# Transpose buffers and queues for the tiles normed as attention ends, the place of q's bias, and the MLP's tile schedule

## The chip, the cores and the metric

The kernel runs on one core of a Trainium2 chip. The metric is the time of one execution on the device, in microseconds (us), as the median of three runs. A core has a matrix engine (TensorE, here PE), three more compute engines (VectorE, DVE; ScalarE, ACT; GpSimd, POOL) and a queue engine (SyncE, SP). Each takes its own instructions in order, and waits for others by semaphores. DMAs are issued by SP, ACT or POOL, and an issue takes time on the queue that issues it. PE's weight loads (PEld) overlap its matmuls.

## The reference

One transformer block with conditioning, in fp32: batch 2, 2048 tokens, 576 channels, 16 heads of 36 channels, an MLP of 2304. Each batch has its own shift, scale and gate rows from a small product with the conditioning vector.

```python
mod = silu(c) @ w_ada + b_ada
sh_msa, sc_msa, g_msa, sh_mlp, sc_mlp, g_mlp = jnp.split(mod, 6, axis=1)
xn = _ln(x, 1e-06) * (1 + sc_msa[:, None, :]) + sh_msa[:, None, :]
qkv = (xn @ w_qkv + b_qkv).reshape(B, N, 3, H, hd)
q, k, v = (qkv[:, :, 0], qkv[:, :, 1], qkv[:, :, 2])
q = _ln(q, 1e-05, qn_g, qn_b)
k = _ln(k, 1e-05, kn_g, kn_b)
attn = softmax(einsum('bqhd,bkhd->bhqk', q, k) * scale)
o = einsum('bhqk,bkhd->bqhd', attn, v).reshape(B, N, C)
x = x + g_msa[:, None, :] * (o @ w_proj + b_proj)
xn2 = _ln(x, 1e-06) * (1 + sc_mlp[:, None, :]) + sh_mlp[:, None, :]
h = gelu(xn2 @ w1 + b1)
return x + g_mlp[:, None, :] * (h @ w2 + b2)
```

## The kernel before

**Stages.** For each of the two batches: `inputs` (norm of x, q, k and v), `attend` (scores, Exp, values) and `outputs` (the projection and the residual). Then the MLP of both batches together: a first product with Gelu in 72 jobs, and a second product. Tokens go in tiles of 128 (16 a batch) and in blocks of 512 (four a batch).

**A normed tile's way to PE.** PE needs the tile with channels on the partitions, so each tile is turned. `tile_turned` (L886) norms the rows (L272 to L279: statistics on DVE, Sqrt on ACT, a reciprocal and a tensor_scalar on DVE). `squares_turned` (L890) transposes 32 x 32 squares on DVE into a tile named `squares` (L893) and writes it with four DMAs (L898) into a DRAM tile `turned`, in which the squares come to stand in their transposed places. `turned_loaded` (L903) reads it back with three DMAs (L906, L908), and `turned_modulated` (L910) applies scale and shift, on ACT (L915, L391, L392) and POOL (L393). There is one `squares` buffer, so a transpose waits until the four DMAs of the tile before have read it.

**inputs** (L941). Tile by tile: the products q and k (L1028 and L1030), then `next_rows(t + 2)` (L1064), which norms and turns the tile two ahead, then the biases of q and k (`biased`, L1065 and L1066), the head norms, and the product v with its bias. DVE's instructions keep the written order here; those of SP, ACT and POOL are ordered by the planner, and DVE's first instructions of batch 1's inputs may come before the last of batch 0's attention.

**attend** (L1104). Scores on PE (L1122), Exp on ACT (L1126, 128x512 a time), values on PE (L1135), which DVE adds into `ot` (L1181 first, L1183 after). In `finish` (L1144) SP writes the row of softmax sums to DRAM (L1149) and reads it back onto 64 partitions (L1150) into `den`; DVE takes the reciprocal (L1154) and multiplies (L1155), and SP copies the result into `qo` (L1160). Hooks run at given steps. Toward the end `rows_opened` loads the rows of the next stage's first tiles, `measure` takes their statistics (L1219), and at the last step `rows_turned` (L1367) calls the `turn` of `rows_begun` (L1206): one Sqrt and one reciprocal for all tiles, then for each tile the tensor_scalar (L1227) and `squares_turned` (L893, L898, on POOL's queue). At the end of batch 0's attention these are two tiles of batch 1, at the end of batch 1's five tiles for the MLP. In attend DVE, POOL and ACT keep the written order, and the hook stands ahead of the last `ot` eviction. The rows lie in `spare` tiles, slices of `kr` (the keys), which is no longer used by then.

**outputs** (L1245). Sixteen tiles in groups of four: the parts of the projection that do not need the last channels come first (`whole`, L409), then those that do (`halved`, L420), then DVE multiplies by the gate (L1259) and adds the residual (L1266), and POOL stores (L1267) and loads (L1254). With batch 1's outputs go the loads of the MLP's first weights: SP issues four `wb` loads (L1443), between them the reads of the five turned tiles (L906, L908), and then `last_rows` (L1451), which DVE casts and splits (L403, L404) between two products of the outputs. Again DVE keeps the written order.

**MLP.** A job is two 128-wide slices of the hidden channels (9 such pairs) for one of eight blocks of 512 tokens: seven products of half blocks (L1537), the last channels (L1551), and on DVE the additions that combine the seven (L1564 to L1571), with a copy (L1563) and Gelu (L1575) on ACT and a store on SP (L1576). Two sets of PSUM banks alternate, so that job j + 2 needs the evictions of job j. `token_sums` (L1504) makes four sums of a block's input, before its first job. `ahead(job)` (L1578) prepares the next block's tiles: tile i of block m + 1 is loaded at job 2i - 4 of block m, normed and turned at 2i - 2, read at 2i and modulated at 2i + 1; block 1's tile 0 is one of the five tiles of attention's end, and its tile 1 is loaded ahead of the first job. Here DVE keeps the written order.

Of the kernel before, what the change touches and what calls it, by code (L numbers as in the profile page):

```python
# [8 lines left out]
F32 = mybir.dt.float32  # L9
# [7 lines left out]
P = 128  # L17
# [14 lines left out]
def dit_block(  # L32
# [25 lines left out]
    nc = tc.nc  # L58
    B, N, C = x.shape
# [7 lines left out]
    NBLK = N // BLK  # L67
    TPB = BLK // P
# [17 lines left out]
    def s_tile():  # L86
        return psum["s"].tile([P, 2, 512], F32, tag="s", name="s")
# [35 lines left out]
    def halves(ap):  # L123
        return ap.rearrange("p (a f) -> p a f", a=2)
# [159 lines left out]
    with psum_pools(), tc.tile_pool(name="ada", bufs=2) as ada:  # L284
# [19 lines left out]
        turned = s_tile()  # L304
# [30 lines left out]
    x1_dram = dram.tile([B, N, C], F32, name="x1_dram")  # L335
# [49 lines left out]
    def affine(which, k, b):  # L385
        return dict(bias=mod[:, which, k, b : b + 1], scale=mod[:, which + 1, k, b : b + 1])
# [368 lines left out]
    def block_of_small():  # L755
# [3 lines left out]
        xs = {}  # L759
# [126 lines left out]
        def tile_turned(xt, queue):  # L886
            rows_normed(xs["pool"], xt, repeated=False)
            return squares_turned(xt, queue)

        def squares_turned(xt, queue):  # L890

            squares = xs["pool"].tile([P, C], F32, name="squares", bufs=1)
            nc.vector.transpose(squares, xt[:, :C])  # L893
            xs["count"] = xs.get("count", 0) + 1
            turned = dram.tile([C, P], F32, name=f"turned{xs['count']}")
            by_square = turned.rearrange("(k d) (g j) -> g d k j", d=SQ, j=SQ)
            for g in range(P // SQ):
                queue.dma_start(  # L898
                    out=by_square[g], in_=squares[g * SQ : (g + 1) * SQ, :].rearrange("p (k j) -> p k j", j=SQ)
                )  # L900
            return turned

        def turned_loaded(dst, cols, turned, queue):  # L903

            full, parts, _ = dst
            queue.dma_start(out=full[:, :, cols], in_=turned[0:512, :].rearrange("(k p) n -> p k n", p=P))  # L906
            for r0 in (0, 64):
                queue.dma_start(out=parts[r0 : r0 + 64, 1, cols].bitcast(F32), in_=turned[512:576, :])  # L908

        def turned_modulated(dst, cols, which, b):  # L910

            full, parts, _ = dst
            for k in range(FULL):
                part = full[:, k, cols]
                nc.scalar.activation(part, part, AF.Identity, **affine(which, k, b))  # L915
            last_modulated(dst, cols, parts[:, 1, cols].bitcast(F32), which, b)

        def input_turned(b, t, queue):
            return tile_turned(tile_loaded(x[b, t * P : (t + 1) * P, :], queue), queue)
# [6 lines left out]
        def input_modulated(b, xnt):  # L926
            turned_modulated(xnt, slice(0, P), 0, b)
            return xnt
# [12 lines left out]
        def inputs(b, weights, work, xnt, rows, loaded):  # L941

            wq, wq4, bq = weights
            normed, squares, taken = {}, {}, []
# [72 lines left out]
            def next_rows(t):  # L1017
                return tile_turned(loaded.pop(0), nc.gpsimd) if loaded else input_turned(b, t, nc.gpsimd)
# [14 lines left out]
            def biased(w, ps, t, both):  # L1033
                bias = halves(bq[:, w * C : (w + 1) * C])
                if w < 2:
                    nc.vector.tensor_tensor(halves(both[:, w * C : (w + 1) * C]), ps[:, :, :HALF], bias, ALU.add)
                else:
                    heads = "p a (h d) -> p a h d"
                    nc.vector.tensor_tensor(
                        vv[:, t, :, 0:HD].rearrange("p (a h) d -> p a h d", a=2),  # L1040
                        ps[:, :, :HALF].rearrange(heads, d=HD),
                        bias.rearrange(heads, d=HD),
                        ALU.add,
                    )
# [4 lines left out]
            for t in range(NT - 2):  # L1049


                both = work.tile([P, 2 * C], F32, name="both", bufs=3)
                turning = b == t == 0
                if turning:
                    q, k = (product(w, xnt, None, (0,)) for w in range(2))
                    for w, ps in enumerate((q, k)):
                        product(w, xnt, ps, (1,))
                    ahead = second_by_feature(rows)
                else:
                    ahead = input_loaded(rows, nc.gpsimd)  # L1060
                    q = product(0, xnt)
                    k = product(1, xnt)
                    input_modulated(b, ahead)
                rows = next_rows(t + 2)  # L1064
                biased(0, q, t, both)  # L1065
                biased(1, k, t, both)  # L1066
                if t > 0:
                    head_scale(t - 1, before)
                v = product(2, xnt)
                biased(2, v, t, both)  # L1070
                if t >= 2:
                    by_feature(t - 2, banks_of_two())
                centred(both)
                before, xnt = both, ahead


            for t in range(NT - 2, NT):
                both = work.tile([P, 2 * C], F32, name="both", bufs=3)
# [125 lines left out]
        spare = [kr[:, c, a * 640 : a * 640 + C] for c in range(4) for a in range(3)]  # L1204

        def rows_begun(tiles):  # L1206

            st = xs["pool"].tile([P, 2, 6], F32, name="st", bufs=2)
            mv = xs["pool"].tile([P, len(tiles), 2], F32, name="mvs", bufs=1)
            rstd = xs["pool"].tile([P, len(tiles)], F32, name="rstds", bufs=1)  # L1210

            def load(i):
                xt, src = tiles[i]
                not_sooner(xt)
                nc.gpsimd.dma_start(out=xt, in_=src)

            def measure(i):
                for a in range(2):
                    nc.vector.bn_stats(st[:, a, :], tiles[i][0][:, a * HALF : (a + 1) * HALF])  # L1219
                nc.vector.bn_aggr(mv[:, i, :], st.rearrange("p a s -> p (a s)"))  # L1220

            def turn():
                nc.scalar.activation(rstd, mv[:, :, 1], AF.Sqrt, bias=eps6)
                nc.vector.reciprocal(rstd, rstd)
                turned = []
                for i, (xt, _) in enumerate(tiles):
                    nc.vector.tensor_scalar(xt, xt, mv[:, i, 0:1], rstd[:, i : i + 1], ALU.subtract, ALU.mult)  # L1227
                    turned.append(squares_turned(xt, nc.gpsimd))
                return turned

            return load, measure, turn
# [79 lines left out]
        for b in range(B):  # L1311
# [43 lines left out]
                (3 + t // NBLK, t % NBLK, 3): lambda t=t: residual_begun(b, t) for t in range(NT + 1)  # L1355
            }
            if b + 1 < B:
                begun = [(spare[9 + t], x[b + 1, t * P : (t + 1) * P, :]) for t in range(2)]
            else:
                begun = [(spare[3 + j], x1_dram[0, j * P : (j + 1) * P, :]) for j in range(TPB + 1)]  # L1360

            def rows_opened():
                opening["begun"] = rows_begun(begun)
# [25 lines left out]
            if b + 1 < B:  # L1389
# [28 lines left out]
        HF = NF // 2  # L1418
        MH = MLP // 2
        PAIR = 2 * P  # L1420
        NB = B * NBLK
# [3 lines left out]
        xnts = [  # L1425
            (
                mx.tile([P, FULL, BLK], F32, name=f"xnt{i}"),
                mx.tile([P, 2, BLK], F32R, name=f"parts{i}"),
                mx.tile([P, P], F32, name=f"tail{i}"),
            )  # L1430
            for i in range(2)
        ]
# [9 lines left out]
        for i, (k, f) in enumerate(((0, 0), (0, 1), (1, 0), (1, 1))):  # L1442
# [4 lines left out]
            for j in (2 * i, 2 * i + 1):  # L1447
                if j <= TPB:
                    n, t = divmod(j, TPB)
# [16 lines left out]
        def mlp_loaded(n, i, queue):  # L1466
            b, blk = divmod(n, NBLK)
            t0 = blk * BLK + i * P
            return tile_loaded(x1_dram[b, t0 : t0 + P, :], queue)

        between = {}
        for j in range(TPB + 1):
            n, i = divmod(j, TPB)
# [104 lines left out]
        def ahead(job):  # L1578


            n, f = divmod(job, HF)

            def at(offset):
                m, g = divmod(job - offset, HF)
                there = m + 1 < NB and g % 2 == 0 and g // 2 < TPB and (m, g) > (0, 0)
                return (m + 1, g // 2) if there else None

            if todo := at(-4):
                rows_ahead[todo] = mlp_loaded(*todo, nc.gpsimd)
            if todo := at(-2):  # L1590
                rows_ahead[todo] = tile_turned(rows_ahead[todo], nc.gpsimd)
            for offset in (0, 1):
                if todo := at(offset):
                    m, i = todo
                    cols = slice(i * P, (i + 1) * P)
                    if offset == 0:
                        turned_loaded(xnts[m % 2], cols, rows_ahead.pop(todo), nc.gpsimd)
                    else:
                        turned_modulated(xnts[m % 2], cols, 2, m // NBLK)

        for m, k, n in ((2, 0, 0), (5, 1, 1), (3, 0, 1), (4, 1, 0)):
            quarter = w2[k * HF * P : (k + 1) * HF * P, n * HALF : (n + 1) * HALF]
# [10 lines left out]
            nc.sync.dma_start(out=hidden[q % len(hidden)], in_=gelus[n][g])  # L1613

        rows_ahead = {}
        rows_ahead[1, 1] = mlp_loaded(1, 1, nc.gpsimd)
        token_sums(0)
        for job in range(0, NB * HF, 2):
            (n0, f0), (n1, f1) = divmod(job, HF), divmod(job + 1, HF)
# [156 lines left out]
```

## Time and profile before

| what | us |
| --- | --- |
| median of three runs | 3218.88 (3217.01 to 3221.77) |
| the profiled execution | 3216.34 |
| its span | 3214.6 |
| PE busy | 3159.8 (98%) |
| DVE busy | 1510.3 (47%) |
| ACT busy | 1515.2 (47%) |
| POOL busy | 673.1 (21%) |
| mean granted TensorE clock | 0.995 of full |

All the views below are of one profiled execution, which took 3216.34; times in them are microseconds from the start of the span. A busy share is an average over all stages. A wait is named after the instruction that waited and the work that released it, with the sum over the places, their number and the longest. The granted clock is a share of TensorE's full speed. The longest parts of PE's time are the values (935.0 for L1135) and the scores (567.9 and 424.0 for L1122); the q, k and v products take 403.8 (L1028). The squares writes are 248 DMAs of 72 KB, 2.3 from issue to landing in the median.

### The profile page before, as it was taken

How to read it: one execution, taken by the hardware profiler on the slowest of the kernel's cores; microseconds unless marked ns; L12 is line 12 of the kernel's file. 1: busy time of each engine (PE TensorE's matmuls, PEld its weight loads, DVE VectorE, ACT ScalarE, POOL GpSimd, SP SyncE). 2: the span in 40 equal slices, each digit the busy share in tenths (PEclk: the TensorE clock that was granted, in tenths of full speed). 3: DMA queues.
4: the chain of work that ended last, by engine and by line, in shares of the span. 5: the costliest groups of instructions: out<-in, count | busy, mean ns of one | idle time of the engine just before them, and what ended most of it. 6: DMA issues, size and time to landing. Idle time of an engine off the chain costs nothing.

```text
span 3214.6 us, 47348 instructions
## 1 busy us (share of the span) xinstructions
PE 3159.8 (98%) x17833; PEld 1895.2 (59%) x17833; DVE 1510.3 (47%) x2213; ACT 1515.2 (47%) x2951; POOL 673.1 (21%) x946
## 2 busy tenths in 40 slices
PE   8999999999999999999999999979999999999999
PEld 6884333333333788633333333347888888777777
DVE  5774333333333477633333333435566554455454
ACT  2436666666666033467666666632555652000000
POOL 4551000121110255300001111032333320111121
PEclk9999999999999999999999999989999999999999
DMA  5222212233221422121222222246544533333331
GB/s 151 73 65 68 77 48 56 62 82 81 70 72 48 156 69 73 39 61 35 48 58 64 62 72 63 66 151 209 159 133 135 145 107 126 138 133 111 118 103 38
DMA packets 150585, 291.51 MB, mean 91 GB/s; under 512 B 29891, under 2 KB 82444, under 8 KB 148236
## 3 DMA queue, kind: packets, MB, share of 16 engines
q1 hardware_dynamic: 105012, 175.48, 17.9%
q0 software_dynamic: 45328, 112.92, 13.4%
q8 instruction: 143, 2.34, 0.3%
q14 instruction: 94, 0.77, 0.1%
q10 hardware_dynamic: 8, 0.00, 0.0%
HBM read 155.42 MB, written 84.63 MB: 75 GB/s over the span
## 4 chain that ended last, share of the span: by engine, by line
PE 95%; DMA 3%; DVE 1%; SPq 0%; ACT 0%; issue 0%; POOL 0%; DVEq 0%; ACTq 0%; POOLq 0%
PE b L1135 28%; PE b L1122 19%; PE s L1688 15%; PE s L1028 11%; PE m L1537 11%; PE s L409 3%; PE m L1551 2%; PE one L1537 2%; PE s L1030 2%; PE s L988 1%; DMA last_rows<-in_w_dram 1%; DMA gelu<-cs 0%; DMA bq<-in_w_qkv_dram 0%; PE s L420 0%; DMA turned<-squares 0%
## 5 line engine op out<-in xcount | busy, mean ns | idle before, releaser
L1126 ACT ACTIVATE pt<-b 128x512 f32<-128x512 f32 x2048 | 1057.7, 608 | 484.9 <-PE b L1135 270.5
L1135 PE MATMUL b<-pt,vt 128*64 128x512 f32 x4096 | 935.0, 598 | 2.4 <-ACT pt L1126 2.4
L1135 PEld LDWEIGHTS b<-pt,vt 128*64 128x64 f32 x4096 | 271.8, 136 | 584.6 <-issue 439.4
L1122 PE MATMUL b<-qm,km 32*128 32x512 f32 x4096 | 567.9, 614 | 0.3 <-DMA km<-qo 0.3
L1183 DVE TENSOR_TENSOR ot<-b,ot 128x512 f32<-128x512 f32 x192 | 132.7, 691 | 643.2 <-PE b L1135 642.8
L1122 PE MATMUL b<-qe,ke 16*128 16x512 f32 x2048 | 424.0, 790 | 0.0
L1028 PE MATMUL s<-wq,xnt 128*128 128x288 f32 x1536 | 403.8, 406 | 4.8 <-ACT xnt L391 2.7
L1688 PE MATMUL s<-ws,as 128*128 128x288 f32 x1440 | 351.8, 406 | 0.0
L1122 PEld LDWEIGHTS b<-qm,km 32*128 32x128 f32 x4096 | 192.0, 184 | 269.9 <-ACT pt L1126 206.3
L1028 PEld LDWEIGHTS s<-wq,xnt 128*128 128x128 f32 x1536 | 280.1, 190 | 66.3 <-ACT xnt L391 2.9
L1688 PEld LDWEIGHTS s<-ws,as 128*128 128x128 f32 x1440 | 273.6, 190 | 75.6
L898 POOL DMA_DIRECT2D turned<-squares x248 | 167.0, 679 | 391.1 <-DVE squares L893 368.4
L1154 DVE RECIPROCAL den<-den 128x512 f32<-128x512 f32 x64 | 213.6, 3337 | 13.8 <-DMA den<-den_dram 13.8
L1537 PE MATMUL m<-xnt,wb 128*128 128x256 f32 x864 | 210.4, 379 | 3.2 <-DVE cs L1571 2.3
L1537 PE MATMUL m<-s,wb 128*128 128x256 f32 x864 | 210.0, 379 | 0.0
L1181 DVE COPY ot<-b 128x512 f32<-128x512 f32 x64 | 44.3, 692 | 332.3 <-PE b L1135 332.3
L1537 PEld LDWEIGHTS m<-s,wb 128*128 128x128 f32 x864 | 164.2, 190 | 22.3
L1122 PEld LDWEIGHTS b<-qe,ke 16*128 16x128 f32 x2048 | 108.4, 184 | 114.5 <-issue 113.2
L1537 PEld LDWEIGHTS m<-xnt,wb 128*128 128x128 f32 x864 | 158.9, 190 | 23.0 <-DVE cs L1571 2.7
L915 ACT ACTIVATE xnt<-xnt,mod 128x128 f32<-128x128 f32 x248 | 102.6, 481 | 138.5 <-DMA xnt<-turned 110.8
L1239 POOL DMA_DIRECT2D kr<-in_x_dram x32 | 17.5, 548 | 715.0 <-DVE met L786 700.2
L1575 ACT ACTIVATE cs<-cs,b_sb 128x512 f32<-128x512 f32 x144 | 98.9, 719 | 115.7 <-DVE cs L1570 94.0
(197 smaller groups left out, 3049.1 us busy)
## 6 DMA issues: line engine op xcount, KB each, us to landing
gelu<-cs SPq DMA_DIRECT2D x144, 256.0 KB
hidden<-gelu SPq DMA_DIRECT2D x16, 2304.0 KB
turned<-squares POOLq DMA_DIRECT2D x248, 72.0 KB, 2.3
den<-den_dram SPq DMA_DIRECT2D x128, 128.0 KB
xnt<-turned POOLq DMA_DIRECT2D x56, 256.0 KB, 3.8
x_dram<-kr POOLq DMA_DIRECT2D x48, 288.0 KB, 2.7
qm<-qo SPq DMA_DIRECT2D x192, 64.0 KB
kr<-in_x_dram POOLq DMA_DIRECT2D x34, 288.0 KB, 3.7
```

The source lines that it names most:

```text
L409: nc.tensor.matmul(outs[a], stationary(k, a), moving(k, a), start=(first and k == 0), stop=(not first and k == FULL - 1),)
L898: queue.dma_start(out=by_square[g], in_=squares[g * SQ : (g + 1) * SQ, :].rearrange("p (k j) -> p k j", j=SQ))
L915: nc.scalar.activation(part, part, AF.Identity, **affine(which, k, b))
L1028: nc.tensor.matmul(out_a, full[:, k, :], wq[:, k, f], start=k == 0, stop=False)
L1122: nc.tensor.matmul(ps, k[r, keys], q[r, :], start=first, stop=not first)
L1126: nc.scalar.activation(pt[:, h, :], banks[2 * c + h], AF.Exp, scale=SCALE)
L1135: nc.tensor.matmul(acc[64 * h : 64 * h + 64, :], vt[:, v0 : v0 + 64], pt[:, h, :], start=pt is pts[0][0], stop=pt is pts[-1][0],)
L1154: nc.vector.reciprocal(den, den)
L1183: nc.vector.tensor_tensor(ot, acc, ot, ALU.add)
L1537: nc.tensor.matmul(out_m[m], wb[:, slot[m], k, f * P : (f + 1) * P], moving[m](k), start=k == 0 and m in (1, 2, 5, 6), stop=k == 1 and m == 1,
L1575: nc.scalar.activation(part, part, AF.Gelu, bias=b1_sb[:, g : g + 1])
L1688: nc.tensor.matmul(ms[m], stationary[m][:, f, :], ws[m][:, f, :], start=(f == 0), stop=(f == HF - 1))
```

## The change

There are three parts.

- `squares_turned` takes a buffer as an argument. The tiles of `rows_begun` are given spare ones: two at the end of batch 0's attention (`spare[7]`, `spare[8]`), five at the end of batch 1's (`spare[8]` to `spare[11]` and `spare[0]`). The four DMAs of tile i are issued by ACT, SP or POOL, as i is 0, 1 or 2 modulo 3. All other tiles use the single buffer and POOL, as before.
- In `inputs` the bias of q comes ahead of `next_rows(t + 2)` on DVE.
- In the MLP tile i is read at job max(0, 2i - 1), so at 0, 1, 3 and 5; it is turned two jobs before that, loaded five before and modulated two after. Ahead of the first job two tiles are loaded and the first of them is normed and turned, before `token_sums(0)`.

```diff
--- before.py
+++ after.py
@@ -887,9 +887,10 @@
             rows_normed(xs["pool"], xt, repeated=False)
             return squares_turned(xt, queue)
 
-        def squares_turned(xt, queue):
-
-            squares = xs["pool"].tile([P, C], F32, name="squares", bufs=1)
+        def squares_turned(xt, queue, squares=None):
+
+            if squares is None:
+                squares = xs["pool"].tile([P, C], F32, name="squares", bufs=1)
             nc.vector.transpose(squares, xt[:, :C])
             xs["count"] = xs.get("count", 0) + 1
             turned = dram.tile([C, P], F32, name=f"turned{xs['count']}")
@@ -1061,8 +1062,8 @@
                     q = product(0, xnt)
                     k = product(1, xnt)
                     input_modulated(b, ahead)
+                biased(0, q, t, both)
                 rows = next_rows(t + 2)
-                biased(0, q, t, both)
                 biased(1, k, t, both)
                 if t > 0:
                     head_scale(t - 1, before)
@@ -1210,7 +1211,7 @@
             rstd = xs["pool"].tile([P, len(tiles)], F32, name="rstds", bufs=1)
 
             def load(i):
-                xt, src = tiles[i]
+                xt, src, _ = tiles[i]
                 not_sooner(xt)
                 nc.gpsimd.dma_start(out=xt, in_=src)
 
@@ -1223,9 +1224,9 @@
                 nc.scalar.activation(rstd, mv[:, :, 1], AF.Sqrt, bias=eps6)
                 nc.vector.reciprocal(rstd, rstd)
                 turned = []
-                for i, (xt, _) in enumerate(tiles):
+                for i, (xt, _, squares) in enumerate(tiles):
                     nc.vector.tensor_scalar(xt, xt, mv[:, i, 0:1], rstd[:, i : i + 1], ALU.subtract, ALU.mult)
-                    turned.append(squares_turned(xt, nc.gpsimd))
+                    turned.append(squares_turned(xt, (nc.scalar, nc.sync, nc.gpsimd)[i % 3], squares))
                 return turned
 
             return load, measure, turn
@@ -1355,9 +1356,12 @@
                 (3 + t // NBLK, t % NBLK, 3): lambda t=t: residual_begun(b, t) for t in range(NT + 1)
             }
             if b + 1 < B:
-                begun = [(spare[9 + t], x[b + 1, t * P : (t + 1) * P, :]) for t in range(2)]
+                begun = [(spare[9 + t], x[b + 1, t * P : (t + 1) * P, :], spare[7 + t]) for t in range(2)]
             else:
-                begun = [(spare[3 + j], x1_dram[0, j * P : (j + 1) * P, :]) for j in range(TPB + 1)]
+                begun = [
+                    (spare[3 + j], x1_dram[0, j * P : (j + 1) * P, :], spare[(8 + j) % len(spare)])
+                    for j in range(TPB + 1)
+                ]
 
             def rows_opened():
                 opening["begun"] = rows_begun(begun)
@@ -1580,23 +1584,25 @@
 
             n, f = divmod(job, HF)
 
-            def at(offset):
-                m, g = divmod(job - offset, HF)
-                there = m + 1 < NB and g % 2 == 0 and g // 2 < TPB and (m, g) > (0, 0)
-                return (m + 1, g // 2) if there else None
-
-            if todo := at(-4):
-                rows_ahead[todo] = mlp_loaded(*todo, nc.gpsimd)
-            if todo := at(-2):
-                rows_ahead[todo] = tile_turned(rows_ahead[todo], nc.gpsimd)
-            for offset in (0, 1):
-                if todo := at(offset):
-                    m, i = todo
-                    cols = slice(i * P, (i + 1) * P)
-                    if offset == 0:
-                        turned_loaded(xnts[m % 2], cols, rows_ahead.pop(todo), nc.gpsimd)
-                    else:
-                        turned_modulated(xnts[m % 2], cols, 2, m // NBLK)
+            def at(**offsets):
+                for i in range(TPB):
+                    read = max(0, 2 * i - 1)
+                    for what, offset in offsets.items():
+                        m, g = divmod(job - read - offset, HF)
+                        if g == 0 and m + 1 < NB and (m, i) > (0, 0):
+                            yield what, (m + 1, i)
+
+            for what, todo in at(turn=-2, read=0, modulate=2, load=-5):
+                m, i = todo
+                block, cols = xnts[m % 2], slice(i * P, (i + 1) * P)
+                if what == "load":
+                    rows_ahead[todo] = mlp_loaded(*todo, nc.gpsimd)
+                elif what == "turn":
+                    rows_ahead[todo] = tile_turned(rows_ahead[todo], nc.gpsimd)
+                elif what == "read":
+                    turned_loaded(block, cols, rows_ahead.pop(todo), nc.gpsimd)
+                else:
+                    turned_modulated(block, cols, 2, m // NBLK)
 
         for m, k, n in ((2, 0, 0), (5, 1, 1), (3, 0, 1), (4, 1, 0)):
             quarter = w2[k * HF * P : (k + 1) * HF * P, n * HALF : (n + 1) * HALF]
@@ -1613,7 +1619,9 @@
             nc.sync.dma_start(out=hidden[q % len(hidden)], in_=gelus[n][g])
 
         rows_ahead = {}
-        rows_ahead[1, 1] = mlp_loaded(1, 1, nc.gpsimd)
+        for i in (1, 2):
+            rows_ahead[1, i] = mlp_loaded(1, i, nc.gpsimd)
+        rows_ahead[1, 1] = tile_turned(rows_ahead[1, 1], nc.gpsimd)
         token_sums(0)
         for job in range(0, NB * HF, 2):
             (n0, f0), (n1, f1) = divmod(job, HF), divmod(job + 1, HF)
```

## The prediction

> **What bounds the kernel now.** First the page: how busy is TensorE?
>
> ```profile
> PE 3159.8 (98%) x17833; PEld 1895.2 (59%) x17833; DVE 1510.3 (47%) x2213; ACT 1515.2 (47%) x2951; POOL 673.1 (21%) x946
> ```
>
> Of a span of 3214.6 us PE idles 54.8, and no other engine is above 47%: the change can win only what PE idles, and what PE's clock loses after idling. So next PE's waits, by the line that waited and what it waited for (sum, times, longest).
>
> ```profile
> PE s L420 <- DVE ot L1183: 14.1, 1, 14.1
> PE s L306 <- DVE x_first L279: 8.4, 1, 8.4
> PE s L420 <- DVE product L1259: 7.6, 2, 4.5
> PE s L409 <- DVE ot L1183: 4.8, 1, 4.8
> PE s L1028 <- ACT xnt L391: 2.7, 1, 2.7
> PE b L1135 <- ACT pt L1126: 2.4, 1, 2.4
> PE m L1537 <- DVE cs L1571: 2.3, 2, 1.5
> ```
>
> L1183 is attention's last eviction, and it keeps PE twice, at the ends of attention: 14.1 in batch 1 (2120.62 to 2134.70), 4.8 in batch 0 (1036.5 to 1041.33). DVE's waits in 2105 to 2185 say why it is late:
>
> ```profile
> DVE squares L893 <- DMA turned<-squares: 17.7, 4, 5.3
> DVE wr L403 <- DMA last_rows<-in_w_dram: 11.3, 1, 11.3
> ```
>
> Four of five transposes wait for the DMAs of the tile before, which must have read the one squares buffer. Then the chain that ended last, over the same stretch (start, duration, what):
>
> ```profile
> 2113.72 2.14 DMA turned<-squares
> 2116.03 0.79 DVE squares L893
> ...
> 2133.29 0.78 DVE squares L893
> 2134.07 0.59 DVE ot L1183
> 2134.99 2.18 DMA den_dram<-ot
> 2137.24 3.57 DMA den<-den_dram
> 2140.83 3.36 DVE den L1154
> ...
> 2153.69 26.24 DMA last_rows<-in_w_dram
> 2179.96 0.76 DVE wr L403
> ...
> 2182.94 1.33 PE s L420 x4
> ```
>
> The eviction stands behind the last transpose, and the chain runs on: last_rows, which SP issues after the softmax's copies and four wb loads, lands at 2179.96 and keeps PE a second time (4.5). Last, stretches just after these stalls (busy time of five engines, then PE's granted clock, DMA share, GB/s):
>
> ```profile
> 2135.00:2139.00 4.00, 4.00 (x11) 2.47 (x10) 0.00 (x0) 1.47 (x4) 2.02 (x4) 0.55 0.70 202
> 2158.00:2162.00 4.00, 4.00 (x13) 2.44 (x14) 3.36 (x5) 0.00 (x0) 1.72 (x4) 0.63 1.02 395
> 2183.00:2187.00 4.00, 4.00 (x11) 2.56 (x12) 3.96 (x3) 0.00 (x0) 0.83 (x2) 0.58 0.47 147
> ```
>
> Four microseconds at 0.55 lose 1.8 more: a stall from 3 us up costs some 2 us beside itself.
>
> **What the skill says.** "TensorE: Matmul & The Clock Gate", HAM oscillation, wants no PE-idle gap above about 3.4 us, or the clock halves. The trace agrees after 14.1, 4.8 and 4.5; it also shows 0.63 after a stall of 3.09, and no dip after 2.7. "DMA: Bandwidth & Descriptors", Issuing engines are not separate DMA queues: more issuing engines save only issue time. Here four issues on POOL take 2.65 and the last lands 2.14 later, so issue is half of such a turn-round. "ScalarE: Activation LUTs", What ACT_TABLE_LOAD costs: 2.66 a switch with its drain; this trace has 1.28 for the load itself.
>
> **The change part by part.**
>
> *A, batch 0's end.* Each tile has a buffer, so the two (L1227, L893) pairs run at 1.32 each from 1031.5 and the eviction ends near 1035, before PE wants it at 1036.5. Tiles 0 and 1 took 15.49 from 1032.38; the same two, undisturbed, took 7.96 in batch 1. Gain 7.5: 4.8 of stall, the rest clock. The four writes that move to ACT and the four to SP find both queues empty there: ACT's next work, the modulates, needs those writes anyway, and SP's next, den's copy, needs the eviction.
>
> *B, q's bias ahead of the next norm.* At 985.25 the scheduler had pulled batch 1's tile-2 norm into batch 0's attention: Sqrt's and then Exp's table load on ACT, and PE waited 2.40 for pt. In the changed program's compiled order this norm stands behind q's bias, which needs PE's product after the outputs, so it cannot be pulled there. Gain 2.4. It then comes two tiles (26.4 us of PE) before its use, and takes about 15: norm with table load 4.07, writes 5.0, read 3.8, modulate. In the other tiles the norm moves behind one DVE instruction, at nothing: PE runs back to back at 13.2 a tile and covers it; without this cover each us late would cost a us in each of 30 tiles. At startup v waited 2.7 for ACT (L391), which stood behind this norm's Sqrt; it then waits for v's weights, still landing near 33. Gain 0.5, between 0 and 2.4.
>
> *C, batch 1's end.* Five pairs back to back from 2110.0: squares ready at 2111.4 to 2116.7, eviction done near 2117.3, before PE's 2120.6. The 14.1 go. What is late next? SP now carries two of the five tiles' writes. The last is issued near 2118.7 (four at 0.5 after 2116.7), lands near 2121, and SP's first read of a turned tile waits for all of them; den's two reloads queue behind it, near 2122.5. Adding 3.57 (den), 3.36 (reciprocal) and 0.76 (multiply): 2130.6, against 2144.98 before, 14 sooner. ACT's eight issues come after its last Exp and Sqrt and before modulates that need these writes: nothing. POOL keeps four issues of twenty and reaches its loads of x sooner: nothing lost. DVE does two products ahead of that reciprocal; both are ready before den lands. SP's following issues (L1160 x5, L908, wb x4) keep their order and lengths, so last_rows is issued near 2140 and lands near 2166.5. PE, from 2110.93 at its undisturbed 18.1 per 4 tiles, arrives near 2157 and waits until 2166.5 + 2.98 (cast, add, product, as from 2179.96 to 2182.94) = 2169.5. From there the end is 28.2 away, as before: 2197.7 against 2211.15. Gain 13.4, not the 14.1 + 7.6 + clock that the waits promise. Bounds: 5 if last_rows' landing is set by traffic rather than by its issue; 27.6 (100.2 less 72.6 undisturbed) if last_rows stops binding.
>
> *D, the MLP's start.* Tile (1,1)'s norm, 2.97 on DVE, now precedes token_sums(0), ending near 2216.2 in the old clock of the trace. PE's m=5 wants the first sum at 2214.71 and gets it near 2216.9: a wait of 2.2. The wait of 1.45 at 2241.72 (a gelu store behind the ws loads) has a fixed end and absorbs as much. Loss 0.8; 3 if the clock dips too.
>
> *E, three places with two norms in a row.* Loading and turning at jobs 0, 1, 3, 5 instead of 0, 2, 4, 6 puts two norms back to back on DVE ahead of the evictions of jobs 16, 34 and 52 (compiled order). The MLP kept its single squares buffer, so the second transpose waits for the first's writes. With T the end of the eviction before: first squares T + 4.07, written 5.0 later (L898 to L906 at 2250.80 and 2280.03), second transpose to T + 9.9, eviction (2.6) to T + 12.4. PE, which ended job 15 some 2.9 before T, has two jobs of 7.0 to do meanwhile and wants this eviction at T + 11.1. Loss 1.3, say 1.5 with the semaphores, three times: 4.5; between 0 and 9.
>
> *Loads one job sooner:* 0. PE's 7.0 a job hides them before and after; no MLP wait names xt.
>
> Sum: -7.5 - 2.4 - 0.5 - 13.4 + 0.8 + 4.5 = -18.5. The profiled execution took 3216.34 (span and 1.7 around it), so 3197.8; the median of the runs lies 2.54 higher: 3200.4.
>
> **The rivals.** *The traffic binds (R1).* last_rows lands 26 after its issue, so bytes, not issue, may set it. For: DMA share 1.02 in 2158 to 2162. Against: until 2135 the share is 0.19, and nothing new is put ahead of it. C gains 5: 3208.8. *No bound left (R2).* The whole 27.6: 3186. For: the DMAs are spread earlier. Against: the 26.24. *The MLP loses it (R3, slower).* E's price is 1.3 + (d - 5.0), d from squares to turned, plus about 2 of clock once the stall passes 3. Slower by over 0.2% needs (23.0 + 6.4)/3 = 9.8 a place, d from 11.5. For: d was 10.75 once, at 2291.85, beside a 2.3 MB hidden load. Against: that load lies near job 11, not at 16, 34 or 52. At d = 13, (1.3 + 8 + 2) x 3 = 33.9 against the 23.0: 3230. *Nothing happens (R4).* The eviction may still end behind something on DVE; against it, no transpose in the changed order waits for a DMA there. 3219.
>
> **How the numbers follow.** Forecast 0.55, R1 0.18, R2 0.12, R3 0.10, R4 0.05. 0.2% is 6.4 us, about what this measurement can tell from no change. Faster: 0.55, 0.12 and 0.15 of R1, so 0.82; R3 is split 0.06 slower, 0.04 within, with R4 and the rest of R1 0.12 within. The forecast's own range is 3192 to 3208 (E 0 to 9, startup, C by 3). With R1 and half of R2 it is 3187 to 3213, which leaves out 0.2.
>
> **What would show it.** A and C: no PE wait on L1184 (the eviction's new line). C: last_rows landing near 2156 on the changed kernel's clock (2166.5 less the 10.4 that A and B win earlier), one PE wait of 10 to 12 on the product at L1260. B: no ACT pt wait. D: PE waits 2 at the first m=5. E: three PE waits of 1 to 2 on cs near jobs 18, 36, 54. Wrong it would be if den's reload on SP is late, if square writes on three queues slow each other, or if a stall above 3 us shows in the MLP.

## The result and the profile after

The changed kernel takes 3206.09 us (median of six, 3201.74 to 3209.03), against 3218.43 (3215.53 to 3221.77) for the kernel before: a ratio of 0.9961, 95% interval 0.9948 to 0.9974. It is 12.3 faster, where 18.5 were forecast; 3206.1 lies inside the stated range of 3187 to 3213, and inside the forecast's own of 3192 to 3208.

In the profiled executions (3209.03, span 3207.2, against 3216.34, span 3214.6) each stage's time can be read from PE's first instruction of the stage to that of the next:

| stage | before | after | difference | forecast |
| --- | --- | --- | --- | --- |
| start, and inputs of batch 0 | 250.5 | 253.2 | +2.7 | -0.5 |
| attention of batch 0 | 781.9 | 780.4 | -1.5 | -2.4 |
| outputs of batch 0 | 79.1 | 71.5 | -7.5 | -7.5 |
| inputs and attention of batch 1 | 999.5 | 999.3 | -0.2 | 0 |
| outputs of batch 1 | 101.1 | 94.5 | -6.6 | -13.4 |
| the MLP's first product | 506.9 | 512.5 | +5.6 | +5.3 |
| its second product | 495.6 | 495.7 | +0.1 | 0 |

These add up to 7.4 and not to 12.3, because the changed kernel's profiled execution is the slowest of its six, 2.9 above their median, and the one of the kernel before lies 2.1 below its median. The first stage differs most from profile to profile: over the nine kernels of this document that have the same code there as the changed one it ended between 249.4 and 253.8. So the medians give the whole, and the profiles say which stage changed.

PE's waits of the changed kernel (sum, times, longest):

```profile
PE s L420 <- DVE product L1260: 17.1, 2, 8.9
PE s L306 <- DVE x_first L279: 8.6, 1, 8.6
PE s L1029 <- DMA wq<-in_w_qkv_dram: 5.5, 2, 3.9
PE m L1541 <- DVE cs L1575: 3.5, 4, 1.5
PE m L1541 <- DVE s L1511: 2.0, 1, 2.0
```

Both waits for attention's last eviction (now L1184) are gone, and so is Exp's. In their place stand two waits at batch 1's outputs, of 8.95 and 8.12, which are not for the eviction but for products that DVE could not reach. DVE's waits over those outputs (2090 to 2185) say why:

```profile
DVE x L1267 <- DMA x<-x_dram: 10.6, 3, 8.9
DVE den L1155 <- DMA den<-den_dram: 10.1, 1, 10.1
DVE wr L403 <- DMA last_rows<-in_w_dram: 9.9, 1, 9.9
```

Nothing waits for squares there any more. The softmax sums `den`, the residual x and last_rows are late instead. The chain that ended last shows where den's lateness begins:

```profile
2109.53 0.79 DVE kr L894
...
2110.68 1.49 SPq L899
...
2113.68 6.00 DMA turned<-kr
...
2120.01 0.39 SPq L907
...
2121.01 0.59 SPq L1152
...
2137.66 27.93 DMA last_rows<-in_w_dram
...
2168.74 1.33 PE s L420 x4
```

SP's square writes take up to 1.9 to issue, and the last lands 6.0 after its issue began. The first read of a turned tile (L907) waits for them, and den's reload (L1152) stands behind that read. The loads of x (L1255) stand on POOL behind the products of the turned tiles (L393), and these wait for the same reads:

```profile
2125.79 0.45 POOL L393 TENSOR_TENSOR parts<-tail,parts 128x128 fp32r<-128x128 f32 x1 [14.21 <-DMA xnt<-turned]
...
2133.76 1.61 POOL L1255 DMA_DIRECT2D x<-x_dram  x3
```

### The profile page after: what moved, and what is told of

Same layout as the page of the kernel before. It is cut to its first block, busy times and chain, and to the rows that moved or that the text cites. A ratio compares the mean times of both kernels' runs of the same rounds, so it can differ in the third digit from the quotient of the medians.

```text
span 3207.2 us, 47334 instructions
## 1 busy us (share of the span) xinstructions
PE 3159.1 (98%) x17833; PEld 1895.6 (59%) x17833; DVE 1510.2 (47%) x2213; ACT 1505.3 (47%) x2941; POOL 657.2 (20%) x922
## 3 DMA queue, kind: packets, MB, share of 16 engines
q0 software_dynamic: 44176, 111.15, 13.4%
## 5 line engine op out<-in xcount | busy, mean ns | idle before, releaser
L1184 DVE TENSOR_TENSOR ot<-b,ot 128x512 f32<-128x512 f32 x192 | 132.7, 691 | 643.3 <-PE b L1136 642.9
L1155 DVE RECIPROCAL den<-den 128x512 f32<-128x512 f32 x64 | 213.5, 3336 | 13.9 <-DMA den<-den_dram 13.9
L899 POOL DMA_DIRECT2D turned<-squares x220 | 147.6, 677 | 222.8 <-DVE squares L894 197.0
L1696 PE MATMUL s<-ws,hidden 128*128 128x288 f32 x576 | 142.3, 406 | 0.0
```

The source lines that it names most:

```text
L899: queue.dma_start(out=by_square[g], in_=squares[g * SQ : (g + 1) * SQ, :].rearrange("p (k j) -> p k j", j=SQ))
L1155: nc.vector.reciprocal(den, den)
L1184: nc.vector.tensor_tensor(ot, acc, ot, ALU.add)
L1696: nc.tensor.matmul(ms[m], stationary[m][:, f, :], ws[m][:, f, :], start=(f == 0), stop=(f == HF - 1))
```

## The experiments

Each has its stages beside it where they matter: "outputs" is batch 1's outputs (101.1 before, 94.5 in the changed kernel), "MLP" its first product (506.9 and 512.5). A stage is read from one profile of each kernel. Kernels with the same code in batch 1's outputs took 93.3 to 95.2 there with the changed kernel's three queues (four kernels), 83.9 to 84.7 with POOL alone (three) and 101.1 to 104.3 with one buffer (three); the MLP's schedule of before took 506.3 to 509.2 (eight). Smaller differences than these say little.

### e1_buffers: own buffers, POOL alone

```diff
- turned.append(squares_turned(xt, (nc.scalar, nc.sync, nc.gpsimd)[i % 3], squares))
+ turned.append(squares_turned(xt, nc.gpsimd, squares))
```

with q's bias and the MLP as before.

> Own transpose buffers at both attention ends, all square writes still on POOL's queue; the rest as before. Theory (the buffer, not the queues, carries the gain): the waits on the last eviction L1184 (14.1 and 4.8) are gone, batch 0's end gains 7.5. In batch 1 twenty issues on POOL take 5 x 2.65 from 1 us after attention's end on PE, the last lands near 16.5 us after it, as late as with three queues (16.5 in the changed kernel), so last_rows lands 61 us after attention's end as there: in all 13 to 15 faster than before, within 2 of the run with three queues. Rival (the queues matter): the reads on SP are later by 4 or more and the gain is 10 or less.

Measured: 3195.82, ratio 0.9936 (0.9922 to 0.9949). That is 21 faster, more than the whole change brings and more than either theory said. Outputs took 84.7, ten less than with three queues; batch 0's outputs took 76.1, 4.6 more. The trace shows something that the expectation had left out: with no square writes on SP, the compiled order of SP is different. SP at batch 1's end (start, duration, what), where PE's attention ended at 2112.11:

```profile
2118.63 0.53 SPq L1151 DMA_DIRECT2D den_dram<-ot  x2
2120.48 1.14 SPq L1152 DMA_DIRECT2D den<-den_dram  x2
...
2132.38 0.53 SPq L1455 DMA_DIRECT2D last_rows<-in_w_dram  x1
2133.29 0.41 SPq L1447 DMA_DIRECT2D wb<-in_w_dram  x1
2133.76 0.45 SPq L907 DMA_DIRECT2D xnt<-turned  x1
```

den goes ahead of all reads of turned tiles, and the planner put last_rows ahead of wb. In the changed kernel, where attention ended at 2104.46, SP has this:

```profile
2106.25 9.34 SPq L899 DMA_DIRECT2D turned<-kr  x8
2115.68 1.81 SPq L1151 DMA_DIRECT2D den_dram<-ot  x2
2120.01 0.39 SPq L907 DMA_DIRECT2D xnt<-turned  x1
2120.45 0.51 SPq L909 DMA_DIRECT2D parts<-turned  x1
2121.01 1.22 SPq L1152 DMA_DIRECT2D den<-den_dram  x2
```

Nor are the writes done much sooner with three queues. Stretches of four microseconds while the writes run, of the changed kernel (the last three columns are PE's clock, DMA share and GB/s):

```profile
2109.00:2113.00 4.00, 4.00 (x19) 2.90 (x19) 1.79 (x3) 0.00 (x0) 2.58 (x5) 1.00 0.97 129
2113.00:2117.00 4.00, 4.00 (x24) 2.94 (x21) 1.42 (x2) 0.00 (x0) 0.00 (x0) 1.00 1.02 223
```

and of e1_buffers:

```profile
2113.00:2117.00 4.00, 4.00 (x18) 3.16 (x17) 3.90 (x7) 0.00 (x0) 4.00 (x7) 1.00 0.55 82
2117.00:2121.00 4.00, 4.00 (x21) 2.89 (x22) 1.51 (x3) 0.00 (x0) 4.00 (x7) 1.00 0.68 106
```

With three queues the sixteen DMA engines are full (share 0.97 to 1.02), and the writes whose landing the profile gives, POOL's four, land 3.6 to 6.1 after the start of their issue, where the twenty of POOL alone take 2.6 in the median. Twenty writes take 14.7 from the first issue to the last landing (2104.97 to 2119.68), against 15.0 for POOL alone (2112.88 to 2127.91).

### e2_ends: part one alone

The buffers and the three queues of the change, all else as before.

> Part one of the change alone: own buffers and three queues. Theory: batch 0's end gains 7.5 and batch 1's end 6.5, as in the changed kernel's trace, 14 in all (3204). SP's eight square writes take 9 us to issue instead of the 4 that were forecast and the last lands 6 us after its issue. Rival (the changed kernel's stages depend on each other): batch 1's end gains the forecast 13.4 here, 21 in all (3197).

Measured: 3201.93, ratio 0.9957 (0.9943 to 0.9971), 15 faster. Batch 0's outputs took 71.5 and batch 1's 94.2: the gain of part one doesn't depend on the other parts, and the rival falls.

### e3_qbias: q's bias alone

```diff
+ biased(0, q, t, both)
  rows = next_rows(t + 2)
- biased(0, q, t, both)
```

> q's bias ahead of the next norm, alone. Theory: no wait of Exp's pt (2.4 gained at batch 0's attention), and at startup v waits for its weights instead of ACT: 3.9 with a clock dip as in the changed kernel's trace, 2.7 lost; no change in all (3218). Rival (that wait for weights differs from run to run and isn't the edit's): startup as before or 0.5 better, 2.4 to 2.9 gained.

Measured: 3215.03, ratio 0.9993 (0.9984 to 1.0001), between the theory and its rival, with an interval that includes no change. Exp's wait of 2.4 is gone and batch 0's attention takes 780.4 instead of 781.9. The startup could not be settled: in the four kernels without this edit the first stage ended at 248.6, 250.1, 250.5 and 254.6 (the last is e1_buffers, which waited 3.5 for the weights too), in the nine with it at 249.4 to 253.8. With the edit, v waited 0.3 to 4.7 for its weights in eight of the nine (in e8_mixed 2.5 for DVE); without it, 2.5 to 2.8 for ACT in three of the four. What the edit costs there is less than the runs differ by.

### e4_mlp: the MLP's schedule alone

The third part of the change's diff and nothing else.

> The MLP's new tile schedule alone, attention ends as before. Theory: 5 slower than before (3223): 2 of wait and 2 of clock at the first job, where the norm is ahead of token_sums, waits of 1.0, 1.0 and 1.5 at the three places with two norms in a row, less the 2.3 of waits that the old schedule had. Rival (these waits come from the changed kernel's other edits): PE's waits in the MLP are those of before, within 1 of it.

Measured: 3224.55, ratio 1.0024 (1.0014 to 1.0035), 7.7 slower. The MLP took 512.1, with the waits of the changed kernel: 1.96 at the first job, then 0.87, 1.01, 0.26 and 0.92 near jobs 18, 36, 38 and 54. So the third part costs by itself what it costs in the whole, some 5. Batch 1's outputs were 3.2 longer too (104.3; e3_qbias had 103.3 with the same code). Batch 0's attention was 1.7 longer as well: after the wait of 2.40 for Exp's pt, which the kernel before has too, the clock dipped here and not there (the last section shows both).

### e5_rows_first: last_rows ahead of wb

From here to e8 the kernels have own buffers and q's bias first, and the MLP's schedule of before.

```diff
+ nc.sync.dma_start(out=last_rows, in_=w1[512:576, :].rearrange("p (a f) -> p a f", a=2))
  for i, (k, f) in enumerate(((0, 0), (0, 1), (1, 0), (1, 1))):
...
- nc.sync.dma_start(out=last_rows, in_=w1[512:576, :].rearrange("p (a f) -> p a f", a=2))
```

> Own buffers, three queues and q's bias as changed, the MLP's schedule as before; on SP last_rows is issued ahead of the four wb loads, all else on SP in the changed kernel's order. Theory (last_rows' place behind 4.6 MB of wb makes the second stall of about 8): that stall and its clock dip are gone, batch 1's outputs take 85 instead of 94.5; the first stall of about 9 stays, since it comes from x's loads and den. Rival (traffic of all kinds sets it): last_rows lands within 3 of before, or the stall only moves to wb, and the outputs take 91 or more.

Measured: 3195.07, ratio 0.9928 (0.9912 to 0.9945). PE's second stall is gone and DVE no longer waits for last_rows. But outputs took 88.3, not 85: the first stall grew from 8.95 to 11.46. DVE's waits there:

```profile
DVE x L1267 <- DMA x<-x_dram: 12.1, 3, 8.5
DVE den L1155 <- DMA den<-den_dram: 10.3, 1, 10.3
DVE wb L1464 <- DMA wb<-in_w_dram: 7.2, 1, 7.2
```

The place of last_rows is worth 6; den and x stay late as they were, and the theory's 85 was missed by 3.

### e6_reads_act: the turned tiles read by ACT's queue

```diff
- turned_loaded(xnts[n], slice(t * P, (t + 1) * P), first[j], nc.sync)
+ turned_loaded(xnts[n], slice(t * P, (t + 1) * P), first[j], nc.scalar)
```

> As the last one, but last_rows behind wb as in the changed kernel, and the turned tiles of batch 1's end read by ACT's queue instead of SP's. Theory (den's reload stands on SP behind the first read, which waits for SP's own slow square writes): den lands about 5 sooner than the 20 us after attention's end of the changed kernel, last_rows is issued 8 or more sooner than its 33 and the outputs take 86 to 90. Rival (SP's eight square writes alone hold den_dram and so den): den within 2 of before and the outputs 92 or more.

Measured: 3197.29, ratio 0.9934 (0.9917 to 0.995); outputs 89.5. The time is the theory's, the mechanism only in part: den was there 17.8 after attention's end, 2.5 sooner and not 5, and last_rows was issued at 31.1, 2 sooner and not 8. Its cast began 21.4 after that issue instead of 27.9; why is not shown. PE had one stall of 14.0 there, while DVE waited 16.0 for x, whose loads stand on POOL behind the work on turned tiles (L393). The rival's part is in den: with the reads off SP, its eight square writes alone kept den_dram until 11.3 after attention's end.

### e7_two_queues: no square write on SP

```diff
- turned.append(squares_turned(xt, (nc.scalar, nc.sync, nc.gpsimd)[i % 3], squares))
+ turned.append(squares_turned(xt, (nc.scalar, nc.gpsimd)[i % 2], squares))
```

> As e6_reads_act with the reads on SP again, but the square writes alternate between ACT and POOL, none on SP. The compiled order of SP is then that of e1_buffers: den's reload ahead of the reads and last_rows ahead of wb. Theory (it is SP's share of the writes and the order that comes with it, not slow writes on hardware queues in themselves): batch 1's outputs take 82 to 86, as e1_buffers' 84.7, the whole 3189 to 3192. Rival (square writes from ACT are as slow as SP's and hold the reads and wb): 89 or more.

Measured: 3194.25, ratio 0.9931 (0.9914 to 0.9947); outputs 87.7. SP has e1_buffers' order here and none of the writes, and the outputs still took 3.0 longer than there. ACT's writes (shortest, median and longest issue in ns, first and last start) and DVE at batch 1's end, where attention ended at 2102.14:

```profile
L899 ACTq DMA_DIRECT2D turned<-kr x12: 309/518/1285, 2102.7 to 2120.4; - x12
```

```profile
2120.08 3.35 DVE L1155 RECIPROCAL den<-den 128x512 f32<-128x512 f32 x1 [11.49 <-DMA den<-den_dram]
```

Twelve writes spread over 18.2 on ACT's queue, but their issues took only 6.5 of it. The rest was waiting: by the trace's semaphores the writes of ACT's third tile waited for den's copy to DRAM (landed at 2111.99), and the last two for den's reload itself (2119.99). den's two reloads, issued at 9.9, were there at 17.9, while in e1_buffers they took from 8.4 to 12.2. POOL was through with its eight writes at 7.4 and sent five loads of 288 KB after them, so that the DMA engines were full while den was under way:

```profile
2110.00:2114.00 4.00, 4.00 (x24) 2.90 (x24) 0.00 (x0) 0.00 (x0) 2.28 (x5) 1.00 0.96 154
2114.00:2118.00 4.00, 4.00 (x18) 3.12 (x17) 0.00 (x0) 0.00 (x0) 0.00 (x0) 1.00 1.01 346
```

In e1_buffers twenty writes at 0.67 each held POOL until 13.9, and the loads behind them came after den had landed. So the rival falls: ACT's writes were not as slow to issue as SP's (up to 1.3, against 1.9), and nothing on SP waited long for them. But the theory's 82 to 86 was missed as well, since den's reload was slow on a queue without any square write. What share POOL's loads and the writes still in flight have in that was not separated.

### e8_mixed: the best stages together

```diff
- turned.append(squares_turned(xt, (nc.scalar, nc.sync, nc.gpsimd)[i % 3], squares))
+ turned.append(squares_turned(xt, (nc.scalar, nc.sync, nc.gpsimd)[i % 3] if len(tiles) == 2 else nc.gpsimd, squares))
```

> Own buffers; three queues at batch 0's end and POOL alone at batch 1's; q's bias first; the MLP's old schedule. Theory (the stages add up): the sum of the best stages measured so far, 19.6 + 232 + 780.4 + 71.5 + 225.7 + 773.7 + 84.7 + 506.5 + 495.6 = 3190 of span, 3191 in time, 26 below the kernel before and 15 below the changed one. Rival (a stage's gain is given back in the next): 3196 or more.

Measured: 3192.18, ratio 0.9916 (0.9899 to 0.9932), 26 below the kernel before and 14 below the changed one. Outputs took 71.5 and 83.9; the stages add up. PE's waits (those over 2):

```profile
PE s L306 <- DVE x_first L279: 8.5, 1, 8.5
PE s L420 <- DVE product L1260: 4.0, 2, 2.1
PE m L1541 <- DVE cs L1575: 2.7, 2, 1.9
PE s L1029 <- DVE rstd L278: 2.5, 1, 2.5
PE s L409 <- DVE product L1260: 2.4, 1, 2.4
```

Set beside each other, in us after attention's end on PE (the first column is the end of the last issue, the other issues are given by their start):

| | last write issued | den reload issued | den there | last_rows issued | its cast begins | outputs |
| --- | --- | --- | --- | --- | --- | --- |
| before | 26.1 | 25.8 | 29.9 | 42.8 | 69.0 | 101.1 |
| after | 11.1 | 16.6 | 20.3 | 33.2 | 61.2 | 94.5 |
| e5_rows_first | 11.3 | 16.8 | 20.5 | 30.4 | 56.5 | 88.3 |
| e6_reads_act | 11.2 | 14.2 | 17.8 | 31.1 | 52.4 | 89.5 |
| e7_two_queues | 18.7 | 9.9 | 17.9 | 26.0 | 53.8 | 87.7 |
| e1_buffers | 13.9 | 8.4 | 12.2 | 20.3 | 47.4 | 84.7 |
| e8_mixed | 14.0 | 7.8 | 11.6 | 19.6 | 46.9 | 83.9 |

### e9_sums_first: token_sums ahead of the norm

```diff
- rows_ahead[1, 1] = tile_turned(rows_ahead[1, 1], nc.gpsimd)
  token_sums(0)
+ rows_ahead[1, 1] = tile_turned(rows_ahead[1, 1], nc.gpsimd)
```

in the changed kernel, all else as changed.

> The changed kernel, but tile (1,1) is turned after token_sums(0). Theory (the norm ahead of the sums delays PE's m=5 by 2.0, and the clock dip after it costs 2 more): the MLP takes 508.6 instead of 512.5 and the whole 3202. Rival (the dip is not that stall's): 510.5, the 2.0 of the wait alone; or, where the norm now delays job 0's eviction, no gain.

Measured: 3210.28, ratio 0.9977 (0.9969 to 0.9986); the MLP took 516.2, 3.7 more than changed. The wait at the first job is gone, but tile (1,1)'s norm now stands next to tile (1,2)'s, ahead of job 0's eviction. DVE there, and then PE:

```profile
2211.64 0.78 DVE L894 STREAM_TRANSPOSE squares<-xt 128x576 f32<-128x576 f32 x1 [5.76 <-DMA turned<-squares]
```

```profile
2214.95 2.63 PE L1541 MATMUL m<-xnt,wb 128*128 128x256 f32 x8 [3.62 <-DVE cs L1575]
```

The edit made a fourth place with two norms in a row, and a dearer one: the DMAs of a square buffer held the transpose for 5.76, and it the eviction. A wait of 2.06 near job 37 came with it, whose origin was not followed. The rival's second half had named the place, but expected no gain, not a loss.

### e10_evict_first: an eviction between the norms

```diff
- ahead(job + 1)
  gelu_stored(n0, f0, 0)
+ ahead(job + 1)
```

> The changed kernel, but in each pair of jobs the first one's evictions are written ahead of the second one's tile work, so that an eviction lies between the two norms on DVE. Theory (the second transpose waits for the first's square writes and holds the eviction): the waits of 1.0, 0.9 + 0.2 and 1.5 near jobs 18, 36 and 54 are gone, the MLP takes 509.0 and the whole 3202.5. Rival (these waits come from gelu's stores, which hold cs): they stay within 0.5.

Measured: 3203.83, ratio 0.9953 (0.9939 to 0.9967). All four waits for cs are gone; of PE's waits in the MLP only those of the first job are left:

```profile
PE m L1541 <- DVE s L1511: 2.0, 1, 2.0
PE m L1541 <- issue: 0.9, 1, 0.9
```

The MLP took 510.0, 2.5 less than changed, where 3.5 were expected. The edit has a price of its own: the first job of six later blocks (jobs 9, 18, 27, 36, 45 and 54) took 7.3 instead of 7.0 to 7.1. The theory stands: two norms in a row were the cause of the waits, and not gelu's stores.

### e11_best: e8_mixed with the mended new schedule

The edits of e8_mixed, e9_sums_first and e10_evict_first on the changed kernel.

> Own buffers, three queues at batch 0's end and POOL alone at batch 1's, q's bias first, and the MLP's new schedule with both mends (sums first, evictions between the norms). Theory (without its two faults the new schedule has none of the old one's waits either): the MLP takes 505, the whole 3189, 2 below e8_mixed. Rival (the old schedule's waits come back with the order restored): 507 to 508, the whole as e8_mixed or above.

Measured: 3193.43, ratio 0.9925 (0.9912 to 0.9939). The MLP took 511.2, not 505: waits of 1.82 and 1.08 on cs as in the old schedule, a clock dip after the first (0.71 and 0.87 in 2218 to 2226), and the 2.0 that e10_evict_first's edit brings in the first jobs of six blocks, 7.3 each against 7.0 in e8_mixed. The rival is right: sooner loads brought nothing, and e8_mixed, with the old schedule, is at least as good.

## Why the prediction was right and where not

- **A, batch 0's end: right.** 7.5 forecast, 7.5 measured. The prediction put all of it down to the buffers, but here the queues have a part: with two tiles the writes are on ACT and SP, and with the same buffers POOL alone took 4.6 more (e1_buffers against e2_ends), with a PE wait of 2.89 and a clock dip at 1075. ACT and POOL did as well as ACT and SP (71.5 in e7_two_queues). In e1_buffers the product that PE waited for stood on DVE behind a cast that waited 14.6 for batch 1's weights; how the queue brings that about was not tested.
- **B, q's bias: right in kind.** The norm left batch 0's attention and Exp's wait of 2.40 went, but a wait of 0.6 for vt came at attention's start; 1.5 net instead of 2.4. The startup term, forecast at -0.5, was +2.7 in this profile and is open: with the same code this stage differs by 4.4 between profiles.
- **C, batch 1's end: half.** The stall of 14.1 went and last_rows became the bound, as said. The term that failed is "issued near 2118.7 (four at 0.5 after 2116.7), lands near 2121". The last tile's four writes on SP took 5.2 to issue instead of 2.0 (0.30, 1.49, 1.42 and 1.90), and the last landed 6.00 after the start of its issue instead of 2.14. So all writes had landed 15.2 after attention's end instead of 10, den was there at 20.3 instead of 15.1 (2122.5 + 3.57), last_rows was issued at 33.2 instead of 29 and took 27.9 instead of 26.2. Of the 6.8 missing in the sum, 5.6 are in last_rows' landing (61.2 against 55.6), and 1.2 in what followed it. Two of the three signs that the prediction had named for being wrong came true: den's reload on SP was late, and the writes slowed each other. It had taken from the Trainium skill ("DMA: Bandwidth & Descriptors", Issuing engines are not separate DMA queues) that more issuing engines save only issue time, and then priced the writes as if they also ran side by side at no cost; here the DMA share was 0.97 to 1.02, and the last landing, counted from the first issue, 0.3 sooner. The 2.14 was also misread: it runs from the start of an issue, so the last write landed 1.5 after POOL was done with it.
- **C, the term that was put at nothing.** POOL "reaches its loads of x sooner: nothing lost" left out what these loads stand behind. They were issued sooner (29.3 after attention's end instead of 38.8), but still behind L393, and DVE waited 8.9 for x: this is PE's first stall of 8.95, where one wait of 10 to 12 was forecast and two came. In the changed kernel the wait for last_rows comes after it and sets the end; in e5_rows_first and e6_reads_act it is the stall that is left (11.46 and 14.0).
- **C, a rounding.** 2122.5 + 3.57 + 3.36 + 0.76 is 2130.2 and not 2130.6, and with the 8.7 that lie in the kernel before between the multiply's end and last_rows' issue "near 2140" is 2138.9. The forecast gave away 1 of gain.
- **R1** gave nearly the number of C (5 against 6.6 measured), by another way: not last_rows' own traffic, which cost 1.7, but the chain ahead of it. **R2's** size was not reached by any kernel: the best outputs took 83.9, and 72.6 would be undisturbed.
- **D, the MLP's start: the wait right, the clock not.** A wait of 1.96 was measured (2.2 forecast), but after it the clock fell to half for 3.41, a loss of 1.7, so that the first job took 10.98 instead of 7.06. The prediction had named that case ("3 if the clock dips too") and not put it into its sum. The waits of the old schedule, 1.45 and 0.89, went, as the absorbing said and 0.9 more: 3.9 - 2.3 = 1.6 net against 0.8.
- **E, two norms in a row: right.** Waits of 0.97, 0.85 + 0.20 and 1.50 at jobs 18, 36 (and 38) and 54 make 3.5, forecast 4.5, and e10_evict_first removed them. d stayed at 4.7 to 5.4 there, so R3's point of 11.5 was far off.
- **The sum.** C's missing 6.8, startup's 3.2, B's 0.9 and the MLP's 0.3 make the profile's 7.4 out of 18.5; the medians, of six executions each, say 12.3. The range held, but the central 18.5 was half as much again as the gain, mainly for C's slow writes.

## What to carry to other kernels

A private buffer took the stall away. Spreading the same twenty writes over three queues made them land hardly sooner (14.7 instead of 15.0), and filled the DMA engines and SP's queue just when one small copy was on the path that sets the end; at batch 0's end, with eight writes, spreading was worth 4.6. So price a moved DMA by what the others in flight do to it, and look at what stands behind it on its new queue: den's reload was issued 16.6 after attention's end behind SP's writes, and 8.4 after it where SP had none. Another queue is no safe place by itself: in e7_two_queues SP had no square write, and den was still there only at 17.9. And when a buffer serves two steps in a row, keep the work that PE waits for between the two steps.

## What was not expected of the hardware

- The issue of a DMA on SP or ACT is not a fixed price. At batch 1's end the same square write took 0.30 to 1.90 on SP (median 0.73 in the changed kernel), 0.31 to 1.44 on ACT there and 0.31 to 1.29 in e7_two_queues, while POOL's stayed at 0.67 to 0.70 in both.
- A PE stall of 1.8 to 2.8 may or may not bring a clock dip. "From 3 us up", as the prediction read it from one trace, is too simple: it matters where the stall lies. The clearest case is one and the same wait of 2.40 for Exp's pt. Here are PE's busy time (the second number) and its clock (the third number from the end) around it, first in the kernel before, then in e4_mlp:

```profile
984.89:988.30 3.41, 2.15 (x24) 0.82 (x17) 2.97 (x9) 2.72 (x4) 0.00 (x0) 1.00 0.31 58
988.30:991.72 3.42, 2.28 (x12) 0.85 (x14) 0.00 (x0) 2.66 (x6) 0.00 (x0) 1.00 0.23 40
991.72:995.13 3.41, 3.41 (x32) 1.34 (x28) 1.63 (x4) 2.61 (x6) 0.00 (x0) 1.00 0.25 82
```

```profile
985.41:988.82 3.41, 1.20 (x6) 0.48 (x8) 0.74 (x2) 2.63 (x5) 0.00 (x0) 1.00 0.29 54
988.82:992.24 3.42, 3.42 (x10) 0.96 (x8) 0.00 (x0) 2.43 (x5) 0.00 (x0) 0.50 0.23 79
```

These stretches follow a grid that the traces themselves give: in each of the thirteen, every fall of the clock to half and every recovery (5 to 13 a trace) lies on steps of 3.413 us, to within 0.004. In the kernel before, the wait is split between two steps, each idle for about a third; in e4_mlp it leaves one step idle for 65%, and the next runs at half clock, a loss of 1.7. Over all thirteen traces, from 27 us on: of 113 full-clock steps that were idle for 5 to 51%, none was followed by one at half; of 12 with 52 to 58%, seven were; of 42 with more than 61%, all were. (In the startup ahead of that, three dips followed steps with 42 to 43%.) The Trainium skill, "TensorE: Matmul & The Clock Gate", The HAM clock gate, gives such a window, 3413 ns long and not reset when a kernel starts; the grid agrees with it.
